# A graph layer on one core: which tile of g, and which piece of the lists, stands beside which block of the adjacency matrix

## The chip, the core and the metric

The kernel runs on one core of a Trainium2 chip. The core has a matrix engine (TensorE, PE in the profile), a vector engine (VectorE, DVE), a scalar engine (ScalarE, ACT), a general engine (GpSimd, POOL), a sequencer that issues transfers (SyncE, SP), and 16 DMA engines between its on-chip memory and the chip's main memory. The metric is the device time of one execution in microseconds (us); lower is better.

## The reference

Inputs are `x` (8 x 4096 x 256), `adj` (4096 x 4096, sparse, non-negative) and a weight `W` (256 x 256), all float32.

```python
HW = einsum('bnf,fo->bno', x, W)
A_norm = relu((adj + adj.T) * 0.5)
D = sum(A_norm, axis=1)
d = where(D > 0, D ** -0.5, 0)
L = eye(N) - d[:, None] * A_norm * d[None, :]
y = relu(einsum('nm,bmo->bno', L, HW))
out = layernorm(x + y)          # over the last axis, eps 1e-5
```

So the adjacency matrix is made symmetric, normalised by its degrees, multiplied with the projected features, and the result goes through a relu, a residual sum and a layer norm.

## The kernel before, in words

Everything with a node index is cut in 32 tiles of 128 rows; the adjacency matrix is cut in 8 x 8 blocks of 512 x 512 (a block is 1 MB). The work has two stages.

The **first stage** (lines 463 to 748) reads the adjacency matrix once. For each row i of blocks and each j from i to 7 it takes the blocks (i,j) and (j,i) together, so that there are 36 steps; a step has two parts, or one on the diagonal. Per part: `load_adj` (L485, on SP's queue) brings the block; `symmetrise` transposes its partner on TensorE (L495) and adds on VectorE (L499) into a tile `sym`; `keep` applies the relu and the half on ScalarE (L503), sums groups of 32 columns on VectorE (L506), marks non-zero groups in `uses` on GpSimd (L507), and writes the part to `a_dram` from ScalarE's queue (L512). When a row is through, its degrees are known and `degrees` makes `r`, the inverse root.

Beside the blocks, the stage forms **g**, the projected and scaled features: 32 tiles, each by `form(m, known)`, which loads 1 MB of x in two halves (L588 on SP's queue, or L554 on GpSimd's where `alone` is set, which it is for rows i >= 4), transposes it (L595), copies it (L596) and multiplies by W (L606). If the degrees of the tile's row are known, the result is scaled by `r` while it is copied (L616), written to `g_dram`, and put in `waiting`: its product with the first column of A (`multiply`, L564, into four banks named `lead`) follows beside the next block. The last ten tiles (22 to 31, `HOLD`) may be formed early, without their degrees (L618); they stay on chip in tiles `held`, and `release` scales and writes them when their row is through. How many tiles are formed beside which block is set before by a sum named `credit` (lines 698 to 708): each off-diagonal block adds 1 and each diagonal one 0.5, twice that from row 4 on; as long as the credit is 1 or more, a tile is formed, a known one first.

The **second stage** (from L885) makes the remaining 31 output tiles in 16 units of two tiles each, gathering only those rows of g which a unit uses. For this it needs **lists**. For unit u, `patterns(u)` computes which of eight groups each row touches (about 16 VectorE instructions), `count` multiplies by matrices of ones on TensorE (L293, L294), `place` (in four pieces, between `yield`s) computes places by a scan and some 45 short VectorE instructions, `count_rest` and `place_rest` (L376, L385 and following) place what is left over, `spread` writes one-hot rows into `hot` (L409, four pieces) and three more operands (L416 to L425), `collect` multiplies them on TensorE (L430), and `index` turns the result into the addresses for the gathers. The lists of the first units of `SEQ` (1, 2, 3, 4) are begun in the first stage; those of units 1 and 2 are brought to their end there (lines 729 to 739). A list `due` holds the pieces with the number of `keep`s to wait, and `run_due` (called after each `keep`) issues what is due. The lists of unit u read the columns of its tiles in `uses`, which are there when the row of blocks that holds these tiles is through.

Instructions are put in order by a scheduler which goes by the program's order and by when buffers are free; the order on each engine is fixed when the kernel is built, and each engine takes its instructions in that order. These buffers matter: four of adjacency blocks (`adj`), three of `sym`, three halves of x (`xin`), four PSUM banks (`b0`) shared by all transposes, g products and list counts. `spread_early` (L679) takes its `hot` tile from the `sym` buffers and its other operands, `mixed`, from the `adj` buffers, and both are held until `collect` has read them.

Of the kernel before, what the change touches and what calls it, by code (L numbers as in the profile page):

```python
# [23 lines left out]
SEQ = [1, 2, 3, 4, 5, 6, 7, 0, *range(8, 16)]  # L24
# [43 lines left out]
def kernel(  # L68
# [31 lines left out]
    NS = N // S  # L100
# [302 lines left out]
    def spread(u, hot, inn, val):  # L403

        at, t = plan[u], tiles[u]
        plan[u] = hot, val
        for m in range(0, NB, NB // 4):
            ms = slice(m, m + NB // 4)
            nc.vector.tensor_tensor(  # L409
                hot[:, ms],  # L410
                iota_q.unsqueeze(1).to_broadcast([P, NB // 4, P]),
                at[:, 1, ms].unsqueeze(2).to_broadcast([P, NB // 4, P]),
                ALU.is_equal,
            )
            yield
        nc.vector.tensor_tensor(  # L416
            inn[:, :, :t],
            iota_q[:, :t].unsqueeze(1).to_broadcast([P, NB, t]),
            at[:, 0, :].unsqueeze(2).to_broadcast([P, NB, t]),
            ALU.is_equal,  # L420
        )
        nc.vector.tensor_tensor(
            val[:, :, 0, :t], inn[:, :, :t], jval.unsqueeze(2).to_broadcast([P, NB, t]), ALU.mult
        )
        nc.vector.tensor_scalar(val[:, :, 1, :t], inn[:, :, :t], iota_p, None, ALU.mult)  # L425
# [44 lines left out]
    with (  # L470
# [12 lines left out]
        def load_adj(i, j):  # L483
            t = blocks_pool.tile([P, A, S], F32, tag="adj", name=f"adj_{i}_{j}")
            nc.sync.dma_start(  # L485
                t,
                adj[i * S : (i + 1) * S, j * S : (j + 1) * S].rearrange("(a p) s -> p a s", p=P),
            )
            return t
# [61 lines left out]
        def load(t, source):  # L551

            with tc.issue_after(loads[-1]) if loads else nullcontext():
                loads.append(nc.gpsimd.dma_start(t, source).ins)  # L554

        def fetch(m):

            t = strips.tile([P, P], F32, tag="strip", name=f"strip_{m}")
            load(t, a_dram[m * P : (m + 1) * P, :P])
            return t  # L560
# [14 lines left out]
        def form(m, known, alone=False):  # L575

            H = B // 2  # L580
            xin = []
            for h in range(2):
                t = xpool.tile([P, H, F], F32, tag="xin", name=f"xin_{m}_{h}", bufs=3)
                source = x[h * H : (h + 1) * H, m * P : (m + 1) * P, :].rearrange("b p f -> p b f")
                if alone:
                    load(t, source)
                else:
                    nc.sync.dma_start(t, source)  # L588
                xin.append(t)
            xt = xpool.tile([P, B, FC, P], F32, tag="xt", name=f"xt_{m}", bufs=1)  # L590
            for b in range(0, B, 2):
                pt = psum.tile([P, 2, FC, P], F32, tag="b0", name=f"xtr_{m}_{b}")
                for k in range(2):
                    for c in range(FC):
                        nc.tensor.transpose(pt[:, k, c, :], xin[b // H][:, b % H + k, c * P : (c + 1) * P], ident)  # L595
                nc.scalar.copy(xt[:, b : b + 2], pt)  # L596
                yield
            if known:
                g = xpool.tile([P, G], F32, tag="g", name=f"gt_{m}")
            else:  # L600
                g = hpool[m].tile([P, G], F32, name=f"held_{m}")
            for b in range(0, B, 2):
                pg = psum.tile([P, 2 * FO], F32, tag="b0", name=f"pg_{m}_{b}")
                for k in range(2):
                    for c in range(FC):
                        ins = nc.tensor.matmul(  # L606
                            pg[:, k * FO : (k + 1) * FO],
                            lhsT=xt[:, b + k, c, :],
                            rhs=w_sb[:, c, :],
                            start=(c == 0),  # L610
                            stop=(c == FC - 1),
                        )
                done_pe.append(ins.ins)
                to = g[:, b * FO : (b + 2) * FO]
                if known:
                    nc.scalar.mul(to, pg, r[:, m : m + 1])  # L616
                else:
                    nc.scalar.copy(to, pg)  # L618
                yield
            if known:  # L620
                nc.scalar.dma_start(g_dram[m * P : (m + 1) * P, :], g)
                waiting.append((m, g, fetch(m)))
            else:
                held[m] = g
# [18 lines left out]


        known, early = [], list(range(NB - HOLD, NB))
        credit = 0.0

        due = [[n + 1, constants, (u,)] for n, u in enumerate(SEQ)]

# [29 lines left out]
        def spread_early(u):  # L679
            hot = spool.tile([P, A, S], F32, tag="sym", name=f"hot_{u}")  # L680
            mixed = blocks_pool.tile([P, A, S], F32, tag="adj", name=f"mixed_{u}")
            mixed = mixed.rearrange("p a s -> p (a s)")
            n = NB * tmax
            return spread(
                u,
                hot.rearrange("p a s -> p (a s)").bitcast(BF16).rearrange("p (m q) -> p m q", q=P),
                mixed[:, : n // 2].bitcast(BF16).rearrange("p (m t) -> p m t", t=tmax),
                mixed[:, n : 2 * n].bitcast(BF16).rearrange("p (m k t) -> p m k t", k=2, t=tmax),
            )

        for i in range(NS):
            diag = stat1.tile([P, A, P], F32, tag="diag", name=f"diag_{i}")
            for j in range(i, NS):
                tij = load_adj(i, j)
                tji = load_adj(j, i) if j > i else tij
                parts = [(i, j, tij, tji)] + ([(j, i, tji, tij)] if j > i else [])
                parts = [(p, spool.tile([P, A, S], F32, tag="sym", name=f"sym_{p[0]}_{p[1]}")) for p in parts]
                credit += (1.0 if j > i else 0.5) * (1 if i < 4 else 2)
                beside = [multiply(*args) for args in waiting]
                waiting.clear()  # L700
                products = len(beside)

                some = i < NS - 2 or i == j
                while some and credit >= 1.0 and (known or early):
                    beside.append(form(known.pop(0), True, i >= 4) if known else form(early.pop(0), False))
                    credit -= 1.0
                    some = i < NS - 2
                credit = min(credit, 1.0)
                for p, sym in parts:
                    for _ in symmetrise(*p, sym):  # L710
                        pass
                if i == NS - 1:


                    release_all(i - 1)
                    beside = beside[products:] + beside[:products]
                for n, b in enumerate(beside):
                    with tc.issue_after(done_pe[-1]) if i == NS - 1 and n < 2 else nullcontext():
                        for _ in b:
                            pass  # L720
                for (rows, cols, _, _), sym in parts:
                    keep(rows, cols, sym, diag)
                    run_due()
            degrees(i)
            diags[i] = diag
            if i != NS - 2:
                release_all(i)
            known += range(i * A, min((i + 1) * A, NB - HOLD))
            if i in (1, 2):
                for n, u in enumerate(SEQ[2 * i - 2 : 2 * i]):  # L730
                    at = 1 + 5 * n
                    due += [[at, patterns, (u,)], [at + 1, count_place, (u,)]]
                    due += [[at + 2 + k, more, (u,)] for k in range(3)]
                    if (i, n) != (2, 1):
                        due.append([at + 5, count_place_rest, (u,)])
            elif i in (3, 4):
                pieces = spread_early(SEQ[i - 3])
                due += [[at, next, (pieces, None)] for at in (1, 2, 3, 3, 4)]
                due.append([5, collect_index, (SEQ[i - 3],)])
            due.sort(key=lambda d: d[0])  # L740
        run_due(True)
        for m in known:
# [142 lines left out]
    with (  # L885
# [102 lines left out]
        u = SEQ[0]  # L988
# [331 lines left out]
```

## Time and profile before

| | us |
|---|---|
| median of 3 runs | 1507.45 (1506.8 to 1508.42) |
| the profiled execution, its own time | 1505.85 |
| its span, first to last instruction | 1503.7 |
| TensorE busy (matmul) | 1387.0 (92% of the span) |
| VectorE busy | 1040.8 (69%) |
| GpSimd busy | 773.3 (51%) |
| ScalarE busy | 361.2 (24%) |
| moved by DMA | 543.04 MB, mean 361 GB/s |

The last part of the first stage ends at 557.7 us of the span (the last L511), and the first products of the second stage in the chain of waits start at 596.87 us. In the lines below, "busy" is the time in which an engine has an instruction at work; ends of matmuls are modelled, so a busy TensorE may still be short of its peak. A share of the DMA engines is that of 16 engines and may come out a little over 1. A group "x32" is 32 instructions of one kind; "<-" names what ended a wait.

### The profile page before, as it was taken

The numbers are of one execution on the slowest core, as the hardware profiler recorded it, in microseconds if no ns is written. First come the engines' busy times: TensorE is split into PE (matmuls) and PEld (weight loads), VectorE is DVE, ScalarE is ACT, GpSimd is POOL, SyncE is SP. The second block draws the span as 40 slices with busy tenths as digits, with TensorE's granted clock in tenths as the row PEclk, the third lists the DMA queues.
The fourth block names the chain that finished last, engine by engine and source line by source line (L and its number), as shares of the span: only waits on it lengthen the run. The fifth ranks groups of instructions, "written<-read, shape, count | busy, mean of one in ns | idle before, by whom it ended". The sixth has DMA issues, their size and how long they took to land.

```text
span 1503.7 us, 29689 instructions
## 1 busy us (share of the span) xinstructions
PE 1387.0 (92%) x11008; PEld 751.7 (50%) x11008; DVE 1040.8 (69%) x3173; ACT 361.2 (24%) x462; POOL 773.3 (51%) x1564
## 2 busy tenths in 40 slices
PE   6999998989999988999999999999999998988983
PEld 5877876767777763343433333333333333433431
DVE  5676668979956462319486897789229897999644
ACT  3555554444444451000101101100010010011111
POOL 3444010011213225775775777777566776777762
PEclk9999999999999989999999999999999999999996
DMA  9999999999989999999999999999979999999994
GB/s 358 366 364 398 399 376 360 367 330 354 356 311 348 332 397 379 394 400 332 373 379 358 375 398 379 382 388 384 366 255 343 343 374 401 374 368 391 379 370 144
DMA packets 217158, 543.04 MB, mean 361 GB/s; under 512 B 19369, under 2 KB 109193, under 8 KB 182425
## 3 DMA queue, kind: packets, MB, share of 16 engines
q0 software_dynamic: 55664, 283.87, 48.8%
q1 hardware_dynamic: 93472, 126.89, 24.6%
q10 hardware_dynamic: 67872, 130.32, 23.1%
q8 instruction: 89, 1.46, 0.4%
q14 instruction: 61, 0.50, 0.1%
HBM read 438.03 MB, written 136.34 MB: 382 GB/s over the span
## 4 chain that ended last, share of the span: by engine, by line
PE 52%; DMA 19%; DVE 19%; issue 5%; POOL 3%; ACT 2%; ACTq 0%; SPq 0%; POOLq 0%; DVEq 0%
PE py L1158 33%; DMA g<-g_dram,gi 9%; PE pg L606 9%; DMA a_dram<-sym 4%; DVE sym L499 3%; PE lead L564 3%; PE tr L495 3%; PE xtr L595 3%; DVE sums L506 3%; DMA ga<-a_dram,ai 2%; DMA xin<-in_x_dram 2%; DVE stats L778 1%; POOL ga L943 1%; DVE xr L769 1%; DVE xr L802 1%
## 5 line engine op out<-in xcount | busy, mean ns | idle before, releaser
L1158 PE MATMUL py<-g,ga 64*32 64x512 f32 (+1 forms) x7136 | 619.9, 609 | 29.1 <-DMA g<-g_dram,gi 24.8
L1158 PEld LDWEIGHTS py<-g,ga 64*32 64x32 f32 (+1 forms) x7136 | 226.9, 113 | 405.7 <-issue 323.2
L951 POOL DMA_INDIRECT g<-g_dram,gi x268 | 306.4, 1143 | 115.7 <-issue 67.4
L943 POOL DMA_INDIRECT ga<-a_dram,ai x268 | 285.9, 1067 | 137.4 <-PE py L1158 65.2
L759 ACT ACTIVATE y<-py,minus_r 128x512 f32<-128x512 f32 x120 | 72.8, 688 | 793.5 <-PE py L1158 562.8
L606 PE MATMUL pg<-w_sb,xt 128*128 128x256 f32 x1024 | 229.5, 382 | 5.8 <-ACT xt L596 4.0
L1158 PE MATMUL py<-g_hub,gh 128*128 128x512 f32 x480 | 222.1, 604 | 3.9 <-DVE pos_k L239 3.9
L499 DVE TENSOR_TENSOR sym<-tr,adj 128x512 f32<-128x512 f32 x256 | 161.5, 680 | 81.1 <-PE tr L495 80.1
L606 PEld LDWEIGHTS pg<-w_sb,xt 128*128 128x128 f32 x1024 | 194.0, 192 | 33.6 <-ACT xt L596 4.4
L507 POOL TENSOR_SCALAR uses<-sums 128x64 uint8<-128x64 f32 x64 | 27.7, 433 | 311.3 <-DVE sums L506 262.8
L506 DVE TENSOR_REDUCE sums<-sym 128x64 f32<-128x2048 f32 x64 | 145.3, 2276 | 51.7 <-ACT sym L503 51.7
L495 PE MATMUL tr<-ident,adj 128*128 128x128 f32 x1024 | 139.7, 287 | 28.6 <-DVE sym L499 16.6
L1158 PEld LDWEIGHTS py<-g_hub,gh 128*128 128x128 f32 x480 | 88.0, 190 | 132.7 <-issue 119.8
L503 ACT ACTIVATE sym<-sym 128x2048 f32<-128x2048 f32 x64 | 122.8, 1918 | 126.5 <-DVE sym L499 126.5
L495 PEld LDWEIGHTS tr<-ident,adj 128*128 128x128 f32 x1024 | 119.7, 147 | 55.3 <-DVE sym L499 34.1
L442 DVE TENSOR_SCALAR low<-lists 128x17 f32<-128x17 f32 (+8 forms) x14 | 2.5, 175 | 197.9 <-PE lists L430 193.3
L769 DVE TENSOR_TENSOR xr<-xr,y 128x2048 f32<-128x2048 f32 x31 | 70.8, 2284 | 52.7 <-ACT y L759 47.1
L595 PE MATMUL xtr<-ident,xin 128*128 128x128 f32 x512 | 73.9, 292 | 14.5 <-DVE sym L499 14.0
L802 DVE TENSOR_SCALAR xr<-xr,mv,root 128x256 f32<-128x256 f32 x248 | 85.6, 416 | 1.1
L778 DVE BATCH_NORM_STATS2 stats<-xr 128x6 f32<-128x256 f32 x248 | 84.1, 412 | 1.1
L564 PE MATMUL lead<-gt,strip 128*128 128x512 f32 x176 | 82.6, 593 | 0.0
L596 ACT COPY xt<-xtr 128x512 f32<-128x512 f32 x128 | 67.9, 593 | 45.1 <-PE xtr L595 44.0
(157 smaller groups left out, 1056.7 us busy)
## 6 DMA issues: line engine op xcount, KB each, us to landing
adj<-in_adj_dram SPq DMA_DIRECT2D x64, 1024.0 KB, 12.1
a_dram<-sym ACTq DMA_DIRECT2D x64, 1024.0 KB, 10.0
out_dram<-xr SPq DMA_DIRECT2D x31, 1024.0 KB, 17.5
xr<-in_x_dram ACTq DMA_DIRECT2D x28, 1024.0 KB, 18.4
xin<-in_x_dram SPq DMA_DIRECT2D x44, 512.0 KB, 10.5
g_dram<-gt ACTq DMA_DIRECT2D x22, 1024.0 KB, 7.6
xin<-in_x_dram POOLq DMA_DIRECT2D x20, 512.0 KB
g_dram<-held ACTq DMA_DIRECT2D x10, 1024.0 KB, 11.7
```

Of the source, the lines that this page charges most:

```text
L495: ins = nc.tensor.transpose(pt[:, c * P : (c + 1) * P], tji[:, c, a * P : (a + 1) * P], ident)
L499: nc.vector.tensor_add(sym[:, a, :], pt, tij[:, a, :])
L503: nc.scalar.activation(sym, sym, AF.Relu, scale=0.5)
L506: nc.vector.tensor_reduce(sums, sym.rearrange("p a (c q) -> p a c q", q=E), AX.X, ALU.add)
L564: nc.tensor.matmul(lead[c], lhsT=strip, rhs=g[:, c * S : (c + 1) * S], start=not done, stop=len(done) == NB - 1, skip_group_check=True,)
L595: nc.tensor.transpose(pt[:, k, c, :], xin[b // H][:, b % H + k, c * P : (c + 1) * P], ident)
L606: ins = nc.tensor.matmul(pg[:, k * FO : (k + 1) * FO], lhsT=xt[:, b + k, c, :], rhs=w_sb[:, c, :], start=(c == 0), stop=(c == FC - 1),)
L778: nc.vector.bn_stats(stats[:, b, :], z[:, b, :])
L802: nc.vector.tensor_scalar(z[:, b, :], z[:, b, :], mv[:, b, 0:1], rstd[:, b : b + 1], ALU.subtract, ALU.mult,)
L943: nc.gpsimd.indirect_dma_start(out=at if both else at[:, : E if one else P], out_offset=None, in_=a_pairs if both else a_groups if one els ...
L951: nc.gpsimd.indirect_dma_start(out=gt, out_offset=None, in_=g_dram, in_offset=bass.IndirectOffsetOnAxis(ap=gi[:, t : t + 1], axis=0), boun ...
L1158: return nc.tensor.matmul(py[2 * u + 1 + b][c][cols, :], lhsT=at[ps, off + cols.start : off + cols.stop], rhs=gt[ps, c * S : (c + 1) * S], ...
```

## The change

Three things change in the first stage; the second stage's program is left as it is.

1. One tile of g (tile 22, an early one) is formed ahead of the first block.
2. The sum `credit` gives way to a function `quota(i, j)` which says how many tiles go beside block (i,j), and whether a known tile is held back in favour of an early one. In rows 0 to 3: one beside each off-diagonal block, but none beside (1,7), and an early one beside (2,7). In rows 4 and 5: one beside each block, two beside (5,6). In rows 6 and 7: one beside the diagonal block. Before, rows 4 and 5 had two beside (4,4), (4,5), (5,5) and (5,6) each and none beside the rest, and row 1 had one beside each of its blocks (the diagonal one too), row 3 one beside each block but (3,7), (3,3) included.
3. The lists are made one unit per row: unit 1 in row 2, unit 2 in row 3, unit 3 in row 4, unit 4 from (5,7) into row 6. Before, units 1 and 2 were made in row 2 and units 3 and 4 in row 3. The spread and collect of unit 1 move from row 4 to the second half of row 3; those of unit 2 stay in row 5.

```diff
         known, early = [], list(range(NB - HOLD, NB))
-        credit = 0.0
+
+        def quota(i, j):
+
+            if i == 2 and j == NS - 1:
+                return 1, True
+            if i == 1 and j == NS - 1:
+                return 0, False
+            if i in (4, 5):
+                return 1 + (i == 5 and j == 6), False
+            return int(i == j if i > 5 else j > i), False
...
+        for _ in form(early.pop(0), False):
+            pass
         for i in range(NS):
...
-                credit += (1.0 if j > i else 0.5) * (1 if i < 4 else 2)
                 beside = [multiply(*args) for args in waiting]
                 waiting.clear()
                 products = len(beside)
 
-                some = i < NS - 2 or i == j
-                while some and credit >= 1.0 and (known or early):
-                    beside.append(form(known.pop(0), True, i >= 4) if known else form(early.pop(0), False))
-                    credit -= 1.0
-                    some = i < NS - 2
-                credit = min(credit, 1.0)
+                forms, held_back = quota(i, j)
+                for _ in range(forms):
+                    if known and not held_back:
+                        beside.append(form(known.pop(0), True, i >= 4))
+                    elif early:
+                        beside.append(form(early.pop(0), False))
...
-            if i in (1, 2):
-                for n, u in enumerate(SEQ[2 * i - 2 : 2 * i]):
-                    at = 1 + 5 * n
-                    due += [[at, patterns, (u,)], [at + 1, count_place, (u,)]]
-                    due += [[at + 2 + k, more, (u,)] for k in range(3)]
-                    if (i, n) != (2, 1):
-                        due.append([at + 5, count_place_rest, (u,)])
-            elif i in (3, 4):
-                pieces = spread_early(SEQ[i - 3])
-                due += [[at, next, (pieces, None)] for at in (1, 2, 3, 3, 4)]
-                due.append([5, collect_index, (SEQ[i - 3],)])
+            if i in (1, 2, 3, 4):
+                u = SEQ[i - 1]
+                at = 4 if i == 4 else 1
+                gap = 2 if i == 1 else 1
+                due += [[at, patterns, (u,)], [at + 1, count_place, (u,)]]
+                due += [[at + 1 + (k + 1) * gap, more, (u,)] for k in range(3)]
+                if i < 4:
+                    due.append([at + 2 + 3 * gap, count_place_rest, (u,)])
+            if i in (2, 4):
+                u = SEQ[i // 2 - 1]
+                at = 4 if i == 2 else 0
+                pieces = spread_early(u)
+                due += [[at + k, next, (pieces, None)] for k in (1, 2, 3, 3, 4)]
+                due.append([at + 5, collect_index, (u,)])
```

## The prediction

> **What bounds the kernel now.** The edit touches only the first stage, so the page's slices come first: the stage fills the first 15 of 40 (37.6 us each).
>
> ```profile
> PE   6999998989999988999999999999999998988983
> DVE  5676668979956462319486897789229897999644
> DMA  9999999999989999999999999999979999999994
> ```
>
> TensorE and the DMA engines are both near nine tenths, VectorE is between five and nine. So I cut the stage at two TensorE marks which the edit leaves in place: the end of the transposes of block (1,7), at 209.3 us, and of (7,7), at 541.7 us. The windows (columns: PE, PEld, DVE, ACT and POOL busy with counts, clock, DMA share, GB/s):
>
> ```profile
> 0.00:209.30 209.30, 190.59 (x1105) 157.81 (x1105) 133.38 (x190) 108.30 (x132) 63.41 (x822) 1.00 1.03 377
> 209.30:310.90 101.60, 87.48 (x473) 69.14 (x472) 91.74 (x239) 46.93 (x53) 11.68 (x25) 0.95 1.01 364
> 310.90:380.90 70.00, 66.85 (x359) 52.35 (x360) 58.81 (x158) 33.88 (x40) 8.34 (x18) 0.98 0.96 347
> 380.90:541.70 160.80, 151.56 (x841) 118.57 (x839) 104.24 (x194) 75.41 (x90) 46.13 (x79) 0.98 0.93 339
> ```
>
> Rows 0 and 1 (first line) are bound by DMA: share 1.03, and VectorE and ScalarE have slack. In row 2 VectorE is 90% busy. In rows 4 to 6 DMA falls to 339 GB/s and TensorE is 94% busy. A limit that changes by row is what an edit of the order can use. Where TensorE stops:
>
> ```profile
> 440.00:460.00 20.00, 14.31 (x107) 11.08 (x106) 16.85 (x32) 7.16 (x7) 4.60 (x8) 0.91 1.03 381
> 460.00:516.00 56.00, 55.48 (x314) 43.51 (x312) 28.51 (x42) 27.38 (x34) 16.99 (x28) 1.00 0.88 321
> ```
>
> and, for the same stretch, the chain of waits:
>
> ```profile
> 437.42 5.15 PE lead L564 x12
> 442.58 0.81 PE pl L430 x32
> ...
> 444.89 2.27 DVE sums L506
> ...
> 447.73 3.79 DVE sym L499 x7
> ...
> 451.83 1.53 DVE sums L506
> ```
>
> Blocks (4,7) and (5,5) follow each other there with no tile of g between, so TensorE waits for VectorE; before and after it, two tiles per block keep TensorE full while DMA drops to 0.88.
>
> **What the Trainium skill says.** "Perfetto Trace Analysis", Optimization Strategy: where the most-contended engine changes over time, interleaving the regimes may help, and equal gaps that repeat can mean that buffers ran out. The windows show such a change. "DMA: Bandwidth & Descriptors", Issuing engines are not separate DMA queues: transfers of all queues run on the same 16 engines, so moving loads to another queue adds no bandwidth; the shares of 1.01 to 1.03 with three queues in use agree. "PSUM — Partial Sum Buffer", Engine vs sequencer instructions: matmuls start and finish in program order and the other queues are strict FIFO. So a form put ahead of a transpose delays it, and list work ahead of a `sym` add delays that; the chain above agrees.
>
> **Prices, from this profile.** Transposes of one part: 1.84 us (3.67 for the 32 of a pair). One tile of g: 1.75 (xtr) + 6.91 (pg) = 8.66. One product into `lead`: 8 x 0.43 = 3.44. A collect 0.9, counts and rests some 0.4. So an off-diagonal block with one tile and one product costs TensorE 15.77. DMA: 4.2 MB of adjacency read and written and 2.15 MB for a tile whose row is known, 6.35 MB; at 380 GB/s 16.7 us, at the 399 of 516 to 541.7 us 15.9. VectorE: four adds at 0.6 spacing, 2.27 and 0.2, 4.8 per part; one unit's lists some 13.5 (row 2, 220.5 to 310.9 us, has 82.9 us of VectorE: less 11 parts and 2.7 for degrees, 27.4 for two units); a spread 4 x 1.21 + 0.83 + 0.83 + 0.41 = 6.9.
>
> **The change, part by part.** Between the marks TensorE has the same work before and after: 36 parts (66.1), 18 tiles (155.9), 19 products (65.4), lists 4.4, in all 291.8 us; before took 332.4, so 40.6 are stalls. DMA bytes between the marks are the same as well. Only stalls can be won.
>
> 1. *The tile ahead of the first block.* Its two loads (2 x 512 KB) go first in SP's queue, ahead of three adjacency loads, and its matmuls ahead of the first transposes, which ran at 7.56 us: they come 8 to 10 us later, and so does the release of the first adjacency buffer, for which the load of block (2,0) waits (it was issued at 11.97). Covered by what is queued: 1.05 MB of x, 3.15 of adjacency, then x of tile 23, adjacency (0,2) and half of tile 24, 6.8 MB, 18 us at 377 GB/s. Without that cover it costs up to 8. Before 209.3 both versions form the same 13 tiles. I take +0.5, range -1 to +6.
>
> 2. *Tile 31 moves from (1,7) to (2,7).* The stretch 209.3 to 241.6, (2,2) and (2,3), is paced by DMA (the chain has an 11.33 us a_dram<-sym in it), and loses 1.05 MB: -2.8.
>
> 3. *(2,4) to (2,6)*, 51.1 us before: list work halves, but 3 x 6.35 MB need 50.1. Take -0.6.
>
> 4. *(2,7) to the transposes of (3,7)*, 292.7 to 380.9, 88.2 us before. (2,7) and (3,3) took 30.2 of it for 18.0 of TensorE work: VectorE ran 26.3 of it, finishing unit 2 and beginning unit 3. Afterwards unit 1 is done by (2,6), and (2,7) has a tile. The stretch now needs 70.6 of TensorE, 72 of VectorE (9 parts of row 3's and (2,7)'s work, unit 2's lists 13.5, the spread of unit 1 6.9, degrees), and 30.5 MB, 80 us at 380. DMA is last: 80, plus 2 for the `sym` pool below: 82.2, so -6.0.
>
> 5. *Rows 4 to 6*, 380.9 to 541.7, 160.8 us with 147.0 of TensorE work and 13.8 of stalls (4 behind VectorE at (4,4), 8.5 around (4,7)). One tile per block closes these. But tile 11 now follows (3,7), not (3,6), with the product of tile 11 behind it: +8.66 + 3.44 = 159.1 of work. With 4.6 of stalls left (DMA 15.9 to 16.7 against TensorE's 15.77 in three blocks; `tot`, `low` and `pl` holding three PSUM buffers at (6,6)) it takes 163.7: +2.9. POOL's queue also carries the loads of x in these rows: each waits for its buffer ahead of a `uses` and of the power of a row's degrees, but the TensorE transposes that free it precede what VectorE sends, so 0; without that cover up to 2 per row.
>
> 6. *Unit 4's last pieces* now stand between `sym` (6,6) and its `sums`, about 10 us of VectorE. Before, VectorE idled there 6.0 and 2.2 us, and product 19 adds 3.44 to TensorE's way to (6,7): hidden. If not, 2 us in the tail.
>
> Sum: +0.5 - 2.8 - 0.6 - 6.0 + 2.9 = -6.0. The profiled execution took 1505.85 us with a span of 1503.7; the span would be 1497.7 and that run 1499.9. The median of the runs is 1.6 above it, so 1501.5.
>
> **Rivals.**
> *DMA floor.* Between the marks 332.4 us at share 0.96, where rows 0 and 1 reach 1.03: 310 would do. If buffers hide all stalls but TensorE's own, half of that 22 is had: 1507.45 - 11.2 = 1496.3. For it: 4 adjacency buffers let loads run two blocks ahead. Against: rows 4 to 6 hold 159 us of TensorE work, whatever DMA does.
> *Given back.* Row 3 now holds the spread and its held buffers, and rows 4 to 6 a tile more: item 4 yields 3 instead of 6, item 5 costs 5, the start 2: -0.4 or so, 1507. For it: TensorE is the bound just where the tile goes.
> *Slower: two `sym` buffers in row 3.* The spread's `hot` takes one of three `sym` buffers from (3,5) to the collect after (3,7). Before, this fell in (4,4) to (4,6), where TensorE needs 27.9 us per block and two are enough. A buffer's round is add 2.4, relu 1.9, queued copies 1.2, landing 10.4 (median of rows 3 and 4; the longest is 14.0): 15.9 per block, just under the 16.5 of DMA. At 14.0 it is 19.5: 3 us more in each of (3,6), (3,7), (4,4), and what comes late there (the transposes of (4,4)) is the head of 159 us of TensorE work. With the start at +6, 1507.45 - 6.0 + 9 + 5.5 = 1516; the buffers alone decide from a landing of some 14, where +9 exceeds the gain: 1510.5.
> *That it doesn't do what it says*: the order built from it has the tile first, one tile per block in row 4 and units 1 to 4 in rows 2, 3, 4 and 5 to 6. No chance given.
>
> **How the numbers follow.** Forecast as summed (1497 to 1504.4) 0.50; DMA floor (below 1497) 0.16; given back (1504.4 to 1510.5) 0.16; slower 0.18. Two runs of this kernel can be told apart from about 0.2%, 3.0 us: faster 0.66, within it 0.16, slower 0.18. The range leaves out less than a tenth at each end: 1491 to 1512; the forecast's own is 1497 to 1504.4.
>
> **What would show it.** Step 1: DMA share stays near 1 from 15 to 30 us and (1,7)'s transposes end within 2 us of 209.3. Step 4: (3,7)'s transposes end near 371.5 to 373, and no TensorE wait for VectorE of over 3 us at (2,7) and (3,3). Step 5: no window in rows 4 and 5 with DMA under 340 GB/s or TensorE under 90%, and 162 to 165 us to the mark at (7,7). The rival in row 3 shows as `sym` adds or `hot` waiting for a_dram<-sym. I am wrong if the first mark moves by over 5 us, or if the second stage, whose program is unchanged, differs by over 3.

## The result, and the profile after

The kernel after takes 1503.22 us (median; 1497.02 to 1509.04), the kernel before, run beside it, 1508.41; the ratio is 0.9961, with a 95% interval of 0.9945 to 0.9976. The forecast was 1501.5 and faster, with 1491 to 1512 as its range. The profiled execution has a span of 1497.7 us, which is the span that the sum of the steps gave. The sum came out to the tenth by chance: the twelve runs of the kernel after spread over 12 us, their median is 5.2 us below that of the kernel before and not 6.0, and below, single steps are off by one to four microseconds, in both directions.

TensorE's slices on the page of the kernel after (each digit is the busy share, in tenths, of a fortieth of the span, here 37.4 us):

```profile
PE   7999979999999989999999999999998999898993
```

The two 8s that the row had in slices 7 and 9 (rows 2 and 3) are now 9s, and slice 6, a 9 before, is a 7. At this grain little more of the first stage can be seen. So I cut the first stage again, this time at the same marks in both kernels and not at round times. The windows of the kernel before (the columns are those of the prediction; the edges are the mark (1,7), the end of the tile of g behind (2,3), that behind (2,6), and the marks (3,7) and (7,7); the first line, 0 to 209.3 us, stands in the prediction):

```profile
209.30:241.60 32.30, 27.11 (x146) 22.95 (x146) 25.68 (x50) 17.17 (x20) 6.17 (x14) 0.89 1.00 354
241.60:292.70 51.10, 49.15 (x272) 38.33 (x271) 48.77 (x148) 25.25 (x30) 2.33 (x5) 1.00 1.02 366
292.70:380.20 87.50, 77.37 (x416) 60.03 (x415) 75.41 (x196) 37.69 (x43) 11.51 (x23) 0.96 0.98 353
380.20:541.70 161.50, 152.26 (x842) 118.75 (x840) 104.94 (x196) 76.11 (x90) 46.13 (x79) 0.98 0.93 340
sum 541.70, PE 496.47 PEld 397.87 DVE 388.18 ACT 264.52 POOL 129.55; mean PE 99.29 PEld 79.57 DVE 77.64 ACT 52.90 POOL 25.91
```

and of the kernel after, between the same five events:

```profile
0.00:207.20 207.20, 189.70 (x1104) 156.31 (x1104) 131.65 (x187) 108.23 (x132) 62.96 (x821) 1.00 1.03 377
207.20:238.70 31.50, 20.28 (x98) 17.17 (x98) 27.48 (x53) 13.13 (x12) 6.42 (x15) 0.78 0.98 359
238.70:288.40 49.70, 48.42 (x267) 38.18 (x266) 42.73 (x102) 25.47 (x30) 2.39 (x6) 1.00 1.04 375
288.40:367.20 78.80, 74.07 (x408) 57.27 (x406) 66.78 (x146) 37.03 (x43) 8.91 (x19) 0.98 0.98 367
367.20:535.00 167.80, 163.37 (x904) 125.89 (x905) 121.46 (x294) 80.57 (x98) 46.44 (x82) 0.99 0.95 347
sum 535.00, PE 495.84 PEld 394.82 DVE 390.09 ACT 264.43 POOL 127.12; mean PE 99.17 PEld 78.96 DVE 78.02 ACT 52.88 POOL 25.42
```

The last lines say the most. TensorE works 496.5 us in the first stage before, and 495.8 after: the work is the same. The stage is 6.7 us shorter (541.7 and 535.0), and 6.1 of it is idle time of TensorE: 45.2 us before, 39.2 after. The rest of the program keeps this: the span is 6.0 us shorter, and the last part of the first stage is written at 551.5 instead of 557.7.

By stretch, with idle time as width less TensorE busy:

| stretch | before: width, idle | after: width, idle | width | idle | forecast of the width |
|---|---|---|---|---|---|
| start to (1,7) | 209.3, 18.7 | 207.2, 17.5 | -2.1 | -1.2 | +0.5 (step 1) |
| (2,2), (2,3) | 32.3, 5.2 | 31.5, 11.2 | -0.8 | +6.0 | -2.8 (step 2) |
| (2,4) to (2,6) | 51.1, 2.0 | 49.7, 1.3 | -1.4 | -0.7 | -0.6 (step 3) |
| (2,7) to (3,7) | 87.5, 10.1 | 78.8, 4.7 | -8.7 | -5.4 | -6.0 (step 4) |
| rows 4 to 6 | 161.5, 9.2 | 167.8, 4.4 | +6.3 | -4.8 | +2.9 (step 5) |

Two later traces of the kernel after, taken on another chip, give 208.6, 31.0, 49.8, 77.9 and 166.6 us for the five widths, and 210.0, 30.6, 49.8, 77.6 and 166.4: the column after repeats within 3 us in the first stretch and within 1.4 in the others. Of the kernel before there is one trace.

Idle time goes from row 3 and from rows 4 to 6 (10.2 us in both), and 6.0 of it comes back in (2,2) and (2,3), where TensorE now has a wait of 5.3 us for the load of an adjacency block. Which waits ended in row 3 is seen in the waits of TensorE in the stretch (2,7) to (3,7), first before, then after (total, times, longest, in us):

```profile
PE tr L495 <- DVE sym L499: 4.2, 4, 2.3
PE pr L376 <- DVE rest L371: 3.2, 1, 3.2
PE xtr L595 <- DVE sym L499: 2.6, 1, 2.6
```

```profile
PE xtr L595 <- DVE sym L499: 3.2, 2, 2.1
PE tr L495 <- DVE sym L499: 0.9, 2, 0.6
PE pr L376 <- DVE rest L371: 0.2, 1, 0.2
```

The transposes waited 4.2 us for VectorE's adds, and 3.2 us stood behind `rest`, VectorE's mark of what the lists left over; both are nearly gone. The third, the x transposes behind an add (they share the PSUM banks), is as it was.

### The profile page after: what moved, and what is told of

Read it like the earlier page. It is cut to its first block, busy times and chain, and to the rows that moved or that the text cites. A ratio compares the mean times of both kernels' runs of the same rounds, so it can differ in the third digit from the quotient of the medians.

```text
span 1497.7 us, 29688 instructions
## 1 busy us (share of the span) xinstructions
PE 1386.5 (93%) x11008; PEld 746.5 (50%) x11008; DVE 1041.9 (70%) x3173; ACT 361.2 (24%) x462; POOL 766.3 (51%) x1564
## 4 chain that ended last, share of the span: by engine, by line
PE 58%; DMA 21%; DVE 13%; issue 3%; ACT 2%; POOL 2%; ACTq 0%; DVEq 0%; POOLq 0%
PE py L1171 34%; PE pg L606 10%; DMA g<-g_dram,gi 9%; PE lead L564 6%; DMA a_dram<-sym 5%; PE tr L495 3%; PE xtr L595 3%; DVE sym L499 3%; DMA xr<-in_x_dram 3%; DMA xin<-in_x_dram 2%; DVE sums L506 1%; DVE stats L791 1%; DMA ga<-a_dram,ai 1%; DVE xr L782 1%; ACT sym L503 1%
## 5 line engine op out<-in xcount | busy, mean ns | idle before, releaser
L1171 PE MATMUL py<-g,ga 64*32 64x512 f32 (+1 forms) x7136 | 623.3, 610 | 32.0 <-DMA g<-g_dram,gi 28.9
L956 POOL DMA_INDIRECT ga<-a_dram,ai x268 | 295.4, 1102 | 139.5 <-PE py L1171 67.6
L964 POOL DMA_INDIRECT g<-g_dram,gi x268 | 292.3, 1091 | 117.9 <-issue 71.3
L606 PE MATMUL pg<-w_sb,xt 128*128 128x256 f32 x1024 | 231.2, 384 | 9.3 <-ACT xt L596 9.3
L606 PEld LDWEIGHTS pg<-w_sb,xt 128*128 128x128 f32 x1024 | 195.2, 193 | 36.7 <-ACT xt L596 10.2
L507 POOL TENSOR_SCALAR uses<-sums 128x64 uint8<-128x64 f32 x64 | 24.4, 381 | 268.5 <-DVE sums L506 222.5
L495 PE MATMUL tr<-ident,adj 128*128 128x128 f32 x1024 | 136.4, 281 | 17.1 <-DVE sym L499 10.9
L495 PEld LDWEIGHTS tr<-ident,adj 128*128 128x128 f32 x1024 | 115.7, 143 | 48.2 <-DVE sym L499 28.7
L596 ACT COPY xt<-xtr 128x512 f32<-128x512 f32 x128 | 68.1, 592 | 61.3 <-PE xtr L595 59.9
## 6 DMA issues: line engine op xcount, KB each, us to landing
xr<-in_x_dram ACTq DMA_DIRECT2D x28, 1024.0 KB, 13.2
xin<-in_x_dram SPq DMA_DIRECT2D x44, 512.0 KB, 11.2
g_dram<-held ACTq DMA_DIRECT2D x10, 1024.0 KB, 10.2
```

Source lines behind the costliest of these rows:

```text
L495: ins = nc.tensor.transpose(pt[:, c * P : (c + 1) * P], tji[:, c, a * P : (a + 1) * P], ident)
L606: ins = nc.tensor.matmul(pg[:, k * FO : (k + 1) * FO], lhsT=xt[:, b + k, c, :], rhs=w_sb[:, c, :], start=(c == 0), stop=(c == FC - 1),)
L956: nc.gpsimd.indirect_dma_start(out=at if both else at[:, : E if one else P], out_offset=None, in_=a_pairs if both else a_groups if one els ...
L964: nc.gpsimd.indirect_dma_start(out=gt, out_offset=None, in_=g_dram, in_offset=bass.IndirectOffsetOnAxis(ap=gi[:, t : t + 1], axis=0), boun ...
L1171: return nc.tensor.matmul(py[2 * u + 1 + b][c][cols, :], lhsT=at[ps, off + cols.start : off + cols.stop], rhs=gt[ps, c * S : (c + 1) * S], ...
```

## The experiments

My theory was that the two halves of the change need each other: a list on its own row only helps if a tile of g stands where TensorE would wait for VectorE, and spreading the tiles only helps if VectorE isn't overloaded elsewhere. The rivals: that the halves add up; that the tile ahead of the first block is worth nothing or harms; that two `sym` buffers in row 3 eat the gain; and that step 5's extra tile behind (3,7) is given away. The first four runs were on one chip, beside one set of runs of before (median 1506.99).

**The lists alone.** The kernel before, with the change's lists (one unit per row) and the credit's tiles:

```diff
-            if i in (1, 2):
-                for n, u in enumerate(SEQ[2 * i - 2 : 2 * i]):
...
+            if i in (1, 2, 3, 4):
+                u = SEQ[i - 1]
...
```

> The kernel before with the new places of the lists alone (one unit per row, spread of unit 1 in row 3); which tile of g stands beside which block stays as it was. Theory A (the parts need each other: lists free VectorE in rows 2 and 3, tiles fill TensorE in rows 4 and 5, and either alone gets less than half): rows 2 and 3 win about 5 us, but unit 3's lists now fall on (4,7) and (5,5), where no tile covers VectorE, and give 3 of it back: ratio to before 0.997 to 1.000, (3,7) transposes about 5 us earlier than before. Theory B (all of the gain is the lists'): 0.995 to 0.996. Theory C (all of it is the tiles'): 1.000, and no mark earlier by over 1 us.

Measured: 1514.17 us, ratio 1.0042 (1.0029 to 1.0056): slower. The gain of row 3 is there: the mark (3,7) comes at 373.9, 6.3 earlier than before. It is lost between the marks (4,7), at 443.7, and (5,5), at 461.2, where before took 3.1 us and this kernel 17.5. The timeline of TensorE there (start, duration, what, and in brackets the idle time before it):

```profile
442.60 1.12 PE L495 MATMUL tr<-ident,adj 128*128 128x128 f32 x4 [2.69 <-DVE sym L499]
457.45 0.21 PE L376 MATMUL pr<-rest,ones 128*128 128x32 bf16 x1 [13.73 <-DVE rest L371]
...
457.55 3.65 PE L495 MATMUL tr<-ident,adj 128*128 128x128 f32 x16
```

After the transposes of (4,7) TensorE's next instruction is the count of what unit 3's lists left over (`pr` from `rest`). It waits 13.7 us for it, and the transposes of (5,5) stand behind it. VectorE wrote `rest` at 457.2. The windows from (3,7) to (4,6), and from there to (5,5), with the lists alone and then in the kernel after, say why it was so late:

```profile
373.90:433.00 59.10, 58.25 (x336) 45.85 (x335) 31.08 (x74) 28.00 (x38) 14.53 (x26) 1.00 0.92 347
433.00:461.20 28.20, 11.69 (x59) 8.72 (x59) 27.44 (x78) 6.73 (x4) 5.47 (x9) 0.66 0.88 308
```

```profile
367.20:415.50 48.30, 46.39 (x279) 36.51 (x280) 32.05 (x76) 23.59 (x30) 12.50 (x23) 1.00 1.00 368
415.50:447.10 31.60, 30.91 (x165) 23.79 (x165) 30.99 (x96) 16.29 (x20) 9.05 (x15) 1.00 1.00 362
```

With the lists alone, the credit puts two tiles beside (4,4) and (4,5) each: 59.1 us in which TensorE is full and VectorE half idle (31.1). Then (4,6) and (4,7), with no tile, bring VectorE the adds and sums of four parts and unit 3's lists at once: 28.2 us in which VectorE is full (27.4) and TensorE works 11.7. In the kernel after, with a tile per block, nearly the same VectorE work (58.5 and 63.0 us over both windows) lies beside more of TensorE's, and in its second window both are full (30.9 and 31.0 of 31.6). What holds the lists back in the first window is TensorE itself: the count of unit 3's groups (`tot`) stands in its order behind the pairs of tiles, and VectorE's scan (`incl_k`) waits for it. VectorE's wait in the first window, with the lists alone and then in the kernel after:

```profile
DVE incl_k L235 <- PE tot L293: 17.8, 1, 17.8
```

```profile
DVE incl_k L235 <- PE tot L293: 5.3, 1, 5.3
```

With the lists alone, VectorE has written what is to be counted (`kind`) by 387.1; the count runs at 426.7, 52.8 us after the mark (3,7). In the kernel after it runs at 409.2, 42.0 us after the mark.

**The tiles alone.** The kernel after with the lists of the kernel before:

```diff
-            if i in (1, 2, 3, 4):
-                u = SEQ[i - 1]
...
+            if i in (1, 2):
+                for n, u in enumerate(SEQ[2 * i - 2 : 2 * i]):
...
```

> The kernel after with the old places of the lists (units 1 and 2 in row 2, 3 and 4 in row 3, spreads in rows 4 and 5). Theory A: 0.997 to 0.999; the stretch from (2,6) to (3,7) gains 4 to 6 us where both changes gain 9.5, rows 4 to 6 lose 5 to 7 as with both. Theory B: 1.000 or slower. Theory C: 0.995 to 0.996.

Measured: 1506.99 us, ratio 1.0003 (0.9987 to 1.0019): no change. (3,7) comes 4.9 us earlier than before, and rows 4 to 6 take 169.1 us instead of 161.5. So lists alone cost 0.42%, tiles alone give nothing, and both together gave 0.39%. If the halves added up, both together would have been some 0.45% slower; that rival is out. (Of the tiles' places, tile 31's move to (2,7) and the tile that (1,1) no longer has were changed only together with the others, so their own shares stay open.) At (3,7) they do about add up (-6.3, -4.9 and, together, -13.0); it is in rows 4 to 6 that they don't (+13.2, +7.6 and, together, +6.3).

**The change without its tiles of rows 4 and 5.** If it is the tile per block that keeps VectorE from falling behind, then putting the pairs back must bring the wait back:

```diff
             if i in (4, 5):
-                return 1 + (i == 5 and j == 6), False
+                return 2 * (j < i + 2), False
```

> The kernel after with the tiles of rows 4 and 5 in pairs again (two beside the first two blocks of each row, none beside the rest). Theory A: TensorE waits for VectorE at (4,7) and (5,5) come back, with unit 3's lists on top, 8 to 14 us more of stalls in rows 4 and 5 than the kernel after: ratio to before 1.001 to 1.005. Rival (rows 4 to 6 are bound by the sum of TensorE's work, whatever its spacing): the same as the kernel after, 0.996.

Measured: 1517.61 us, ratio 1.0065 (1.0047 to 1.0083). (3,7) is at 367.6, within 0.5 us of the kernel after; (7,7) at 555.3 is 20.3 later. TensorE's timeline behind (4,7), at 450.7:

```profile
464.76 0.21 PE L376 MATMUL pr<-rest,ones 128*128 128x32 bf16 x1 [14.06 <-DVE rest L371]
```

It is the same wait, 14.1 us. In the kernel after, TensorE's timeline at this place reads:

```profile
433.86 1.91 PE L595 MATMUL xtr<-ident,xin 128*128 128x128 f32 x16
435.61 7.07 PE L606 MATMUL pg<-w_sb,xt 128*128 128x256 f32 x32
442.52 0.18 PE L376 MATMUL pr<-rest,ones 128*128 128x32 bf16 x1
...
442.57 1.07 PE L495 MATMUL tr<-ident,adj 128*128 128x128 f32 x8
```

A tile (x transposes and `pg`) stands before the count, which doesn't wait. VectorE had written `rest` at 433.1, so that 9 us were to spare. It is thus not that the tile fills the wait: a tile of 8.66 us wouldn't fill 14. `rest` is written 66 us after the mark (3,7) in the kernel after, 83 with the lists alone (457.2 less 373.9) and 97 here (464.5 less 367.6); the count comes 42, 53 and 67 us after the mark. So most of the delay is there before VectorE's scan begins: tiles spread over the blocks let the count run earlier, and VectorE has its time for the list.

**Without the tile ahead of the first block** (it goes back beside (1,7), as an early one):

```diff
             if i == 1 and j == NS - 1:
-                return 0, False
+                return 1, True
...
-        for _ in form(early.pop(0), False):
-            pass
         for i in range(NS):
```

> The kernel after without the tile ahead of the first block; its number of early tiles is kept by one beside (1,7). If the tile ahead fills DMA at the start (the mark at (1,7) came 2.1 us earlier with it) and one tile less stands at (1,7): 2 to 3 us slower than the kernel after, ratio to before 0.997 to 0.998. Rival (the tile ahead is bought with a late start of the transposes and gives nothing): the same as the kernel after, 0.996.

Measured: 1499.92 us, ratio 0.9945 (0.9923 to 0.9967), beside 0.9961 for the kernel after: no loss. Its mark (1,7) comes 3.7 us earlier than the kernel after's, with one tile fewer formed before it, and its mark (7,7) 2.5 us later. A second pair of traces, further below, had 2.9 us at (7,7) in the same direction. I took this for a small worth of the tile, which the next two runs were to settle.

All other runs fell to another chip, on which the kernel before takes 1741 us; the first stage is as long there (the kernel after reaches (7,7) at 533.9 and 534.4), so marks can be compared with those above, but ratios only with those taken beside them.

> The kernel after without the tile ahead of the first block (the same kernel as in the run without the first tile), beside the kernel after on one chip. Two pairs of traces have put the tile ahead at 2.5 and 2.9 us less at the mark (7,7): if this reaches the end, this kernel is 2 to 3 us slower than the kernel after (ratio some 0.002 higher). If it is lost in the second stage, as the first timing had it (0.9945 beside 0.9961), the two ratios lie within 0.002 of each other or this one is lower.

> The kernel after itself, beside the one without the first tile: ratio 0.994 to 0.998, as measured twice (0.9961 and 0.9955).

Measured: without the first tile 1733.15 us, ratio 0.9941 (0.9916 to 0.9966); the kernel after 1734.42, ratio 0.9968 (0.9949 to 0.9986). And (7,7) came at 529.1 without the first tile, 5.3 earlier than with it: the sign that I had read from two pairs of traces was wrong. The same kernel without the first tile reached (7,7) at 537.5 in one execution and 529.1 in the other, one on each chip (the kernel after at 535.0, 533.9 and 534.4); the difference begins in rows 1 to 3, which DMA paces. A single trace's mark can thus be off by as much as 8 us. What stands is the timing: twice the kernel without the tile ahead was no slower than the kernel after, by the ratios 0.0016 and 0.0027 faster, with intervals that overlap. It beats the kernel before in both; that it beats the kernel after isn't shown. A third pair, with another tile moved in both (the two runs with the tile back at (3,3), below), has the kernel without the tile slower by 0.0006. The tile ahead of the first block gives nothing that can be measured.

**The tile behind (3,7) put back to (3,3).** This asks what step 5 paid:

```diff
                 return 1 + (i == 5 and j == 6), False
+            if i == 3:
+                return int(j < NS - 1), False
             return int(i == j if i > 5 else j > i), False
```

> The kernel after, with one tile of g beside the diagonal block (3,3) and none beside (3,7): a tile (8.66 us of TensorE) and the product behind it (3.44) are back ahead of the transposes of (3,7), as they were before. It measures what step 5 charged to rows 4 to 6. If those rows are bound by TensorE and row 3 has room beside its DMA (it had 9.2 us of idle TensorE from 288.4 to 535.0 us in all), the mark (3,7) comes 4 to 7 us later than in the kernel after (367.2), the stretch to (7,7) takes 154 to 158 instead of 167.9, and the end is 4 to 8 us earlier: ratio to before 0.991 to 0.994. If the stalls only move to row 3, where VectorE and DMA are at nine tenths, (3,7) comes 10 to 13 later, (7,7) within 2 of 535.0, ratio 0.995 to 0.998. If the work of VectorE at (3,3) is what the tile gets in the way of, it is over 0.998.

> The kernel after itself, on the same chip and beside the same runs of before as the three others, so that differences of one or two us between them can be read: ratio 0.9945 to 0.9976 as measured before, mark (7,7) within 1 us of 535.0.

Measured: 1737.82 us, ratio 0.998 (0.996 to 1.0), beside 0.9955 (0.9933 to 0.9977) for the kernel after. Between the marks (3,3) and (3,7), and then (7,7), first with the tile back at (3,3), then in the kernel after (the first window of the former begins 6.8 us before the mark):

```profile
306.00:384.10 78.10, 72.53 (x389) 57.98 (x388) 58.06 (x120) 37.21 (x44) 10.71 (x20) 0.96 0.93 336
384.10:542.80 158.70, 152.80 (x853) 116.19 (x852) 120.52 (x292) 75.06 (x90) 45.21 (x79) 1.00 0.96 353
```

```profile
307.70:367.30 59.60, 54.78 (x301) 41.33 (x300) 52.32 (x111) 28.14 (x32) 4.89 (x12) 1.00 0.98 366
367.30:533.90 166.60, 162.15 (x905) 124.67 (x905) 121.66 (x295) 80.67 (x98) 47.42 (x82) 1.00 0.95 349
```

From (3,3) to (3,7) it takes 71.3 us (384.1 less 312.8) instead of 59.6, from there to (7,7) 158.7 instead of 166.6. So 12.1 us of TensorE's work cost 11.7 in row 3 and 7.9 in rows 4 to 6, where part of it lies in what had been idle. Against the kernel after, (7,7) comes 8.9 us later, but 5.1 of that is there at (3,3), ahead of the edit. The expectation of a gain was a miss. The second one, that the stalls only move, has the ratio (0.998 is its edge) and, with the 5.1 taken off, the 10 to 13 at (3,7); (7,7) is 3.8 later, not within 2. The same edit without the first tile, too:

> The kernel after without the tile ahead of the first block (it goes back beside (1,7), an early one) and with the tile of row 3 beside (3,3) instead of (3,7). If the two gains add: the end 4 to 8 us earlier than without the first tile alone (0.9945), ratio 0.989 to 0.992. If they don't: 0.993 to 0.997.

Measured: 1739.89 us, ratio 0.9986 (0.9965 to 1.0006), beside 0.9955 for the kernel after. (Its (7,7), at 545.8, is the one that lay 2.9 us behind its pair, at 542.8.) There was no gain to add to another. The tile stands better behind (3,7), or no worse; both ratios are above the kernel after's, by 0.0025 and 0.0031, with intervals that overlap a little.

**The spread of unit 1 put back to row 4.** This frees the third `sym` buffer in row 3:

```diff
-            if i in (2, 4):
-                u = SEQ[i // 2 - 1]
-                at = 4 if i == 2 else 0
+            if i in (3, 4):
+                u = SEQ[i - 3]
+                at = 0
                 pieces = spread_early(u)
```

> The kernel after, with the spread and collect of unit 1 in row 4 as before; the rest of the lists stays as changed. The rival of two sym buffers in row 3 at the price it was given (3 us in each of (3,6), (3,7), (4,4)): (3,7) comes 6 to 9 us earlier than in the kernel after, (7,7) some 6, ratio 0.990 to 0.993. From the waits of the trace (0.65 and 1.62 us for a landing in row 3) it should give 2 to 3 us at (3,7), and rows 4 to 6, with 6.9 us more of VectorE's work beside unit 3's lists, take that back: (7,7) within 3 us, ratio 0.995 to 0.998. If VectorE becomes the bound in row 4: (4,7) 4 to 8 us later, ratio up to 1.001.

Measured: 1736.77 us, ratio 0.9965 (0.9943 to 0.9988), beside 0.9955 for the kernel after: no gain. (3,7) comes at 366.8, 0.5 earlier than in the kernel after taken beside it, not the 6 to 9 of the rival's price. Between (5,5) and (5,6) it takes 20.8 us instead of 13.9, with 3.4 of idle TensorE in them, and there VectorE's waits show the `sym` buffers in a place that I had not thought of:

```profile
DVE hot L409 <- DMA a_dram<-sym: 3.6, 1, 3.6
```

Unit 2's first `hot` waits 3.6 us for a landing before it gets its buffer, and all that stands behind it on VectorE waits too. So holding a `sym` buffer costs little in row 3; in this run it costs more in row 5, where unit 2's spread has stood in all these kernels.

**The pair of tiles of row 5 moved by one block** (without the first tile), to see whether (5,6) is the pair's fault:

```diff
-                return 1 + (i == 5 and j == 6), False
+                return 1 + (i == 5 and j == 7), False
```

> The kernel after without the first tile, and with the two tiles of row 5 beside (5,7) instead of (5,6). At (5,6) of the kernel after TensorE waited 1.8 us for a copy on ScalarE's queue, behind a relu, behind adds that waited for a sym buffer; the whole of rows 4 to 6 held 4.4 us of idle TensorE. If that place was the pair's, the mark (7,7) comes 2 to 4 us earlier than without the move, and the ratio is 0.001 to 0.003 lower. If the wait follows the unit's spread, which holds a sym buffer from (5,5) to (5,7), nothing changes: within 1.5 us at (7,7).

Measured: 1733.74 us, ratio 0.9956 (0.9937 to 0.9975), beside 0.9941: no gain. The waits of TensorE for a copy (L606 on L596) are 2.5 us with the pair at (5,7) as they are with it at (5,6) in the kernel after. The mark (7,7) is 4.8 us later than without the move, of which 2.5 are there at (5,6), ahead of the edit; so the rest is less than what a single trace can tell. The wait doesn't follow the pair. That it follows the spread fits, but was not tried by itself.

## Why the prediction was right, step by step

*The sum* was right: -6.0, and the span went from 1503.7 to 1497.7, to the tenth by luck. So was its basis, that the work of the stage is the same and only stalls can be won (496.5 and 495.8 us of TensorE). The sizes of the terms were less good, and some readings were off. The mark (3,7) of the kernel before is at 380.2 and not at 380.9, so that step 4's 88.2 us are 87.5 and step 5's 160.8 are 161.5. And the stalls are too large: between the marks (1,7) and (7,7) the prediction's own windows have 305.9 us of TensorE busy (87.48, 66.85 and 151.56), not the 291.8 of its count, so 26.5 us are idle and not 40.6; at (2,7) and (3,3) it is 21.9 busy and not 18.0.

*Step 1*, +0.5: the first transposes came 7.5 us later (18.7 instead of 11.2; 8 to 10 forecast), and by the block (1,2) this was gone; the share of DMA from 15 to 30 us is 1.06 in both. The mark (1,7) came 2.1 us earlier, and in the two later traces of the same kernel 0.7 earlier and 0.7 later. DMA stayed busy, as the cover had it. That the step is worth nothing, the runs without it show.

*Step 2*, -2.8, came to -0.8. What failed is "loses 1.05 MB": two halves of x less are issued there (1.05 MB), but by rate times width the stretch moved 11.4 MB before (354 GB/s in 32.3 us) and 11.3 after (359 in 31.5). SP's queue moved 0.5 MB less and ScalarE's 0.4 more: what is moved between two marks of TensorE is not what is issued there. DMA did pace the stretch (0.98): TensorE had a tile less to do and stood idle instead, +6.0, of which 5.3 is one wait for a load.

*Step 3*, -0.6, came to -1.4, with 0.7 less of TensorE's work in it and 0.7 less idle time.

*Step 4*, -6.0, came to -8.7. It moved fewer bytes: 28.9 MB (367 in 78.8) instead of the 30.5 MB of the step and the 30.9 of before (353 in 87.5). They were not loaded ahead, for up to 288.4 us the kernel after had moved 108.1 MB and the kernel before, up to 292.7, 109.0. They went behind the mark: one adjacency block, two halves of x and one write of g, about 3 MB, are issued in rows 4 to 6 instead, which move 58.2 MB instead of 54.9. The step took 380 GB/s and 2 us for `sym`; 28.9 at the measured 367 is 78.8 by itself. The mechanism was right in the main: the waits for `rest` and for adds went, and DMA is at 0.98. That DMA alone is last isn't shown: TensorE is busy 74.1 of the 78.8, and its waits that are left are for VectorE. The mark (3,7), said to come at 371.5 to 373, came at 367.2. Of the -8.7, 3.3 is TensorE work that now stands behind the mark (77.4 and 74.1 busy; a product is 3.44), and 5.4 is idle time. Steps 2 and 4 together were forecast at -8.8 and came to -9.5.

*Step 5*, +2.9, came to +6.3. Its stalls were right in size: 4.4 us of idle TensorE are left, where I said 4.6. That is luck, as they are not in the places that I gave. TensorE waits for no load in these rows, and from 480 us to (7,7), which takes in (6,6), it doesn't wait at all; it waits 2.5 us for copies on ScalarE and 1.9 for adds. What was mis-sized is "147.0 us of TensorE work", a count of instructions times the durations of undisturbed groups. The window has 152.3 us busy before (151.56 in the prediction's own). The other 5 us I had booked as stalls that one tile per block would close, but in them TensorE had matmuls at work, spread out, and it still has. The x transposes of the tiles show it, in rows 4 to 6 before and after (count, busy us, mean ns):

```profile
L595 PE MATMUL xtr<-ident,xin 128*128 128x128 f32 x144 | 20.0, 289 | 3.4 <-DVE sym L499 3.3
```

```profile
L595 PE MATMUL xtr<-ident,xin 128*128 128x128 f32 x163 | 21.2, 276 | 1.7 <-DVE sym L499 1.6
```

At the price of 1.75 a tile, nine tiles (144) would be 15.8 and ten 17.5 (163 has three of the next). One tile and one product are added. TensorE's busy time rises by 11.1 in all (12.1 forecast), its idle time falls by 4.8. With 152.3 as its base the same step gives 152.3 + 12.1 + 4.6 = 169.0; the stretch took 167.8. The criteria for it (162 to 165, no window under 340 GB/s) were missed for the same reason, and for a second one, the two tiles beside (5,6). The windows of row 5 in the kernel after:

```profile
445.00:460.00 15.00, 15.00 (x85) 12.09 (x84) 12.93 (x24) 6.50 (x9) 4.43 (x9) 1.00 1.04 397
460.00:480.00 20.00, 18.19 (x86) 13.78 (x85) 8.97 (x12) 10.35 (x14) 5.42 (x10) 0.91 0.87 315
480.00:500.00 20.00, 20.00 (x106) 15.69 (x105) 10.66 (x21) 9.09 (x12) 4.48 (x6) 1.00 0.73 241
```

Where before had 14.31 us of TensorE in 20 around (4,7), the kernel after is full until 460 (15.00 in 15.00), and DMA with it (1.04). The idle DMA has moved on: 0.87 and 0.73 from 460 to 500 us, behind the pair.

*Step 6* and the second stage: the stage's end keeps 6.2 us of the 6.7, the span 6.0. Nothing of unit 4's last pieces shows. From (7,7) to the end of the span it takes 962.0 us before and 962.7 after, within the 3 us that were set.

*The rivals.* "DMA floor": rows 4 to 6 are held by 163.4 us of TensorE in 167.8, as was said against it. "Given back": rows 4 to 6 took back 6.3, more than its 5, but row 3 won 8.7 and not 3. (Its terms, with those of steps 2 and 3, add up to +0.6 and not to -0.4, so it stands for 1508.) "Slower" by two `sym` buffers in row 3: the adds wait there for a landing 2.3 us in two times, and TensorE 0.2 and 1.1 us behind them; the run with the spread in row 4 gains 0.5 at (3,7). So the mechanism is real, but small where it was priced at 9, and row 5 has it too. It shows in part of the chain of waits of the kernel after at (5,6), in order of time (start, us, what):

```profile
453.20 8.88 DMA a_dram<-sym
...
462.27 2.50 DVE sym L499 x4
...
464.84 0.69 ACT sym L503
...
465.57 0.37 ACTq L512
...
466.66 0.58 ACT xt L596
467.28 8.86 PE pg L606 x32
```

A landing of 8.88 us frees the buffer; the adds run; the relu follows on ScalarE, then the issue of a write, and only then the copy of x, which has stood in the same queue behind the relu, and which TensorE needs for `pg`. TensorE waits 1.8 us. The Trainium skill's "PSUM — Partial Sum Buffer", Engine vs sequencer instructions (queues other than TensorE's are strict FIFO), which the prediction drew on for VectorE, holds for ScalarE here: two things that have no data in common are tied by their order in a queue. With 8.88 us of landing it is cheap; I had said that it decides at some 14, which no run here tests.

What the prediction did not see is how much hung on the tile per block in rows 4 and 5. Step 5 says "One tile per block closes these" of 8.5 us around (4,7), and gives unit 3's lists, which are new in row 4, no price. That is right only because the tiles are spread in the same change: with pairs the lists cost 14 us in one piece, and the kernel is 0.65% slower than before. What the spread tiles save was not priced without them, as it was for the first tile's cover. The Trainium skill's "Perfetto Trace Analysis", Optimization Strategy, says that interleaving regimes may help where the most contended engine changes; here it has a number: the two windows of the lists alone are a stretch of TensorE and one of VectorE, one after the other (59.1 and 28.2 us), and the kernel after covers the same blocks in 79.9, with 7.4 us more of TensorE's work in it.

## What to carry to other kernels

Before an instruction that waits for another engine is moved, look at how busy that other engine is around the new place, block by block, and at what it waits for in its turn: the same list added no wait where TensorE's work was spread evenly over the blocks and 14 us where it stood in pairs, so the two moves are one change and must be measured as one (here -0.39% together, +0.42% and 0 apart). Take the work of a stretch from the busy column and not from count times duration, and its bytes from rate times width and not from what is issued in it: here 1.05 MB less were issued in a stretch, and 0.1 less moved. And 3 us can't be read from the marks of one trace each: the same kernel's mark moved by 8 between two executions, one on each chip.

## What the hardware showed

The same kernel after took 1503.22 us on one chip and 1734.42 on another, and the kernel before 1508.41 and 1741.18. The first stage took as long on both (535.0 and 534.4 us to the mark (7,7)); the difference is in the second. A window of it, on the first chip and on the other:

```profile
600.00:900.00 300.00, 297.47 (x2902) 116.94 (x2901) 185.62 (x697) 21.81 (x36) 207.27 (x204) 1.00 0.99 375
```

```profile
600.00:900.00 300.00, 244.97 (x2115) 85.89 (x2108) 129.76 (x501) 14.52 (x24) 151.81 (x154) 0.91 0.78 283
```

On the other chip DMA is busy 0.78 of the time instead of 0.99 and moves 283 GB/s instead of 375, TensorE stands idle 55 us in 300, and its granted clock is 0.91 instead of 1.00. The second stage gathers rows by index, the first moves whole blocks. Which comes first there, late gathers or the clock, none of these runs tells; and as all runs on the second chip came after those on the first, that the chip makes the difference isn't shown either. The change's gain, made in the first stage, was found on both: 0.9961 on the one, 0.9955 and 0.9968 on the other.
